# Two cross-attention layers on one core: the scores of a group issued ahead of the maxima in each slot

## The chip, the cores and the metric

The kernel runs on one core of a Trainium2 chip. The metric is the device time of one execution in microseconds. A core has engines that run side by side, each with its own in-order queue: TensorE (PE in the profile, its weight loads PEld), VectorE (DVE), ScalarE (ACT), GpSimd (POOL), and SyncE (SP), which issues most DMAs. They wait for each other by semaphores. Results of TensorE land in PSUM, which the kernel uses as eight banks of 128 partitions by 512 fp32 values, and are read from there by ScalarE or VectorE.

## The reference

Two residual cross-attention layers on the same hidden states, 32 samples of 256 rows by 320 channels, with 77 context rows of 512 channels and 20 heads of 16 channels. In the shapes at hand the layers' object, other and image-prompt parts are cut out of an empty rest of the context, so that what is left of each layer is:

```python
q = heads(x @ wq); k = heads(ctx @ wk); v = heads(ctx @ wv)   # 20 heads of 16
s = einsum('bhqd,bhkd->bhqk', q, k) / sqrt(16)
p = softmax(s, axis=-1)
x = merge(einsum('bhqk,bhkd->bhqd', p, v)) @ wo + bo + x
```

All of it is fp32.

## The kernel before

**Units and groups.** A unit is one layer for one pair of samples: 16 pairs, two layers, 32 units (`units_in_order`). A unit's 20 heads by 2 samples are worked through in five groups of eight (`NG = 5`, g = 0 to 4); the channels stand on the partitions, so a group's scores come out with the 77 keys on the partitions.

**The steps of a unit,** with the names that the profile uses for their tiles:
- `queries` and `outputs_and_queries` (tiles psq, and psy for the output projection of the unit three before), `keys` and `keys_rest` (psk), `vals` (psv): projections. `mask_keys`, `split_keys`, `split_queries` prepare operands on POOL; `spread_keys` and `spread_queries` move them over the partitions by DMA (kS, qs).
- `maxima`: the row maximum for the softmax. TensorE computes scores with the queries on the partitions (psm, line 500; four banks for up to three halves of a group), VectorE reduces each bank (m, line 512). Each unit has ten halves. They are computed some slots ahead of the scores of the same unit, so the maxima of a slot belong to a later unit than its scores.
- `turn`: the ten halves' maxima are split in high and low parts and transposed on VectorE (maxes, mT, lines 532 to 535), then spread by DMA into `max_rows`.
- `scores`: four banks pss. First a matmul that subtracts the maxima (line 550, written "less" below, `pss<-max_rows,less`), then sixteen with the split keys and the queries (line 558), then four exponentials on ScalarE (pT, line 564).
- `values`: `products` multiplies the exponentials of a group with the values (po, line 578, one bank); `divide` transposes po on VectorE (turned, line 590), takes the reciprocal of the sums (inv, line 594) and multiplies on POOL (normal, line 599). `turn_back` transposes the result into oT on VectorE (line 613).
- `add` (line 620) adds bias and residual on VectorE.

**The ring of banks.** All PSUM tiles come from one pool of eight buffers with one tag, in the order of the calls of `bank`. A tile takes the buffer of the tile eight allocations earlier, and its first matmul waits until that one has been read.

**The order.** The order of the instructions is written out by hand. `at(slot, where, step)` notes a step for a slot; at the end the slots are gone through one by one, and in each slot the kinds of step in the order of a tuple; every engine's queue follows this order. Slots 0 to 134 hold the groups: `slot_of(u, g)` gives the slot of a group's scores, its values stand in the slot behind, and its transpose back (g below 4) one later. Four units take 17 slots; units 1, 2 and 3 of each four have their groups 0 and 1 in one slot (a two-score slot), the fourth has one group in its first slot. The maxima are dealt out in order to the slots with a single group: three halves a slot, two in two slots of each 17, none in the two-score slots. Projections of keys and values ("rest" and "full") stand behind the values, one or two in most slots; I call what stands behind po its tail. The paired output and query projection stands at the end of a unit's first slot. Slots below zero are the start-up.

Of the kernel before, what the change touches and what calls it, by code (L numbers as in the profile page):

```python
# [95 lines left out]
def xattn_kernel(ctx: ExitStack, tc: tile.TileContext, xT, cT, cP, weights, outT):  # L96
# [566 lines left out]
    def slot_of(u, g):  # L663
        if u == NU - 2:
            return start(u) + (g + 1) // 2
        if u == NU - 1:
            return start(u - 1) + 3 + g // 2
        return start(u) + (max(0, g - 1) if u % 4 else g)
# [10 lines left out]
    for u, (p, layer) in enumerate(units):  # L679
# [38 lines left out]
        for g in range(NG):  # L718
            slot = slot_of(u, g)
# [65 lines left out]
    for u, slot in ((1, 1), (2, 4)):  # L785
# [7 lines left out]
    at(3, "load", lambda: load_weights(1, "v", "v", nc.sync))  # L793
    at(4, "load", lambda: load_weights(1, "o", "b", nc.sync))

    order = (
        "load", "maxima", "turn back", "scores", "values", "rest", "back", "turn", "split", "full", "last",
    )
    for slot in range(min(s for s, _ in place), max(s for s, _ in place) + 1):
        for where in order:  # L800
            for step in place.get((slot, where), ()):
                step()

# [97 lines left out]
```

## Time and profile before

| | |
|---|---|
| median of 3 runs | 944.42 us (943.32 to 945.34) |
| the profiled execution | 947.08 us |
| its span in the profile | 945.3 us |
| mean granted TensorE clock in it | 0.998 |
| instructions | 48848 |
| matmuls | 21582 |
| VectorE reductions of the maxima, mean | 512, 551 ns |
| ScalarE exponentials, mean | 640, 593 ns |
| VectorE transposes of po, mean | 160, 684 ns |
| VectorE transposes back, mean | 160, 431 ns |

A row of the profile's timeline gives the start and the length in us, the engine, the line, the operation, out<-in, its shape, how many instructions are merged in it, and in brackets the idle time ahead of it with what ended it. A row of the waits gives "engine line waited for: us in total, times, longest". The ends of matmuls are modelled and overlap, so the distance between the starts of successive matmuls says more about TensorE than their lengths; four matmuls on different rows or columns of the array start within 0.02 us and run side by side.

### The profile page before, as it was taken

To read this page: it belongs to the slowest core of one execution; us is meant where nothing else is said; L and a number is where in the kernel's file an instruction comes from. 1 tells how busy PE (TensorE), PEld (TensorE's weight loads), DVE (VectorE), ACT (ScalarE), POOL (GpSimd) and SP (SyncE) were. 2 spreads that over 40 slices of the span, in tenths; PEclk is the share of its full clock that TensorE was granted. 3 is DMA by queue.
4 is the path that set the end of the run, shared out by engine and by line. 5 is a ranking of instruction groups with operands and counts; after the bars stand their busy time and mean duration, and the time that the engine had idled before them with its cause. 6 is when DMAs were issued, how large, how long until landed. Compare 5 with 4: busy or idle time off the path is not lost.

```text
span 945.3 us, 48848 instructions
## 1 busy us (share of the span) xinstructions
PE 926.6 (98%) x21582; PEld 640.8 (68%) x21582; DVE 574.5 (61%) x1330; ACT 432.0 (46%) x975; POOL 406.9 (43%) x608
## 2 busy tenths in 40 slices
PE   8999999999999999999999999999999999999998
PEld 6666667766667666666766677666767666676654
DVE  4475557655577565665656666665566654776575
ACT  2254443644435534355443545335454354444462
POOL 2354445434455434455234454344553335543431
PEclk9999999999999999999999999999999999999999
DMA  6664444253453525536245352355433543353342
GB/s 227 196 217 129 133 147 145 82 172 120 163 153 95 197 76 163 165 104 201 68 145 176 98 201 82 125 175 161 153 96 120 160 155 119 92 162 105 118 136 97
DMA packets 114740, 133.03 MB, mean 141 GB/s; under 512 B 47012, under 2 KB 76004, under 8 KB 114530
## 3 DMA queue, kind: packets, MB, share of 16 engines
q1 hardware_dynamic: 113666, 127.42, 42.8%
q8 instruction: 170, 2.79, 1.3%
q10 hardware_dynamic: 864, 2.49, 0.7%
q14 instruction: 40, 0.33, 0.1%
HBM read 35.39 MB, written 10.49 MB: 49 GB/s over the span
## 4 chain that ended last, share of the span: by engine, by line
PE 88%; DVE 7%; DMA 2%; SPq 1%; issue 1%; POOL 0%; ACT 0%; POOLq 0%
PE psy L203 15%; PE po L578 15%; PE psq L203 14%; PE psm L500 10%; PE psv L203 7%; PE pss L558 7%; PE psk L203 7%; PE psy L237 4%; PE pss L550 4%; PE psq L237 3%; DVE m L512 3%; DVE turned L590 1%; PE psk L344 1%; DVE maxes L533 1%; SPq L316 1%; DMA x<-in_xT_dram 1%
## 5 line engine op out<-in xcount | busy, mean ns | idle before, releaser
L564 ACT ACTIVATE pT<-pss 77x512 f32<-77x512 f32 x640 | 324.4, 593 | 171.7 <-PE pss L558 171.0
L512 DVE TENSOR_REDUCE m<-psm 128x6 f32<-128x462 f32 (+2 forms) x512 | 248.3, 551 | 221.4 <-PE psm L500 220.9
L599 POOL TENSOR_TENSOR normal<-turned,inv 128x256 f32<-128x256 f32 x160 | 99.3, 621 | 484.5 <-DVE inv L594 457.5
L578 PE MATMUL po<-pT,v 77*32 77x256 f32 x2560 | 166.8, 385 | 8.3 <-DVE m L512 5.2
L203 PE MATMUL psy<-oT,w 128*32 128x256 f32 (+1 forms) x3072 | 164.5, 379 | 0.0
L203 PE MATMUL psq<-x,w 128*32 128x256 f32 (+1 forms) x3072 | 153.4, 380 | 0.6 <-DMA w<-in_w_dram 0.6
L203 PEld LDWEIGHTS psy<-oT,w 128*32 128x32 f32 (+1 forms) x3072 | 88.4, 108 | 63.4 <-issue 15.2
L590 DVE STREAM_TRANSPOSE turned<-po 128x512 f32<-128x512 f32 x160 | 109.5, 684 | 24.4 <-PE po L578 24.3
L203 PEld LDWEIGHTS psq<-x,w 128*32 128x32 f32 (+1 forms) x3072 | 86.8, 109 | 54.9 <-issue 2.2
L274 POOL TENSOR_SCALAR kT<-kR,masks 128x154 f32<-128x154 f32 x186 | 113.3, 619 | 19.2 <-ACT kR L333 19.2
L578 PEld LDWEIGHTS po<-pT,v 77*32 77x32 f32 x2560 | 72.4, 109 | 69.6 <-DVE m L512 26.7
L500 PE MATMUL psm<-kT,q 32*128 32x154 f32 x2560 | 116.2, 306 | 2.3 <-POOL kT L274 2.0
L500 PEld LDWEIGHTS psm<-kT,q 32*128 32x128 f32 x2560 | 90.1, 183 | 35.3 <-issue 25.3
L279 POOL TENSOR_TENSOR halves<-q,halves 128x512 fp32r<-128x512 f32 (+1 forms) x93 | 102.1, 1098 | 7.8
L558 PE MATMUL pss<-qs,kS 32*77 32x256 f32 x2560 | 104.6, 276 | 0.0
L620 DVE SCALAR_TENSOR_TENSOR x<-psy,w,x 128x256 f32<-128x256 f32 x160 | 68.3, 476 | 50.6 <-PE psy L203 49.2
L558 PEld LDWEIGHTS pss<-qs,kS 32*77 32x77 f32 x2560 | 89.2, 141 | 11.3
L613 DVE STREAM_TRANSPOSE oT<-normal 128x256 f32<-128x256 f32 x160 | 67.0, 431 | 45.8 <-POOL normal L599 45.8
L203 PE MATMUL psv<-w,cv 128*32 128x160 f32 x2432 | 93.5, 299 | 0.2 <-DVE m L512 0.2
L418 ACT COPY q<-psq 128x256 f32<-128x256 f32 x28 | 10.4, 372 | 161.8 <-PE psq L237 161.8
L203 PEld LDWEIGHTS psv<-w,cv 128*32 128x32 f32 x2432 | 77.8, 110 | 4.4 <-DVE m L512 0.6
L550 PE MATMUL pss<-max_rows,less 32*77 32x512 f32 x640 | 78.7, 468 | 1.4 <-DMA max_rows<-mT 1.4
(48 smaller groups left out, 725.3 us busy)
## 6 DMA issues: line engine op xcount, KB each, us to landing
qs<-halves SPq DMA_DIRECT2D x256, 128.0 KB
kS<-k_halves SPq DMA_DIRECT2D x128, 192.5 KB
c<-in_cP_dram SPq DMA_DIRECT2D x32, 308.0 KB
cv<-in_cT_dram SPq DMA_DIRECT2D x38, 256.0 KB
out_dram<-x SPq DMA_DIRECT2D x15, 640.0 KB
x<-in_xT_dram SPq DMA_DIRECT2D x14, 640.0 KB
qs<-halves SPq DMA_DIRECT2D x128, 64.0 KB
v<-stage SPq DMA_DIRECT2D x26, 192.5 KB
```

The costliest lines, as they stand in the source:

```text
L203: nc.tensor.matmul(out[m : m + 32], lhsT[:, m : m + 32], rhs, **flags)
L274: engine.tensor_scalar_mul(kT[:, e], kR[:, groups], masks[:, e : e + 1])
L279: engine.tensor_tensor(low, x, high.bitcast(F32), ALU.subtract)
L500: nc.tensor.matmul(ps[j][:, i * 2 * L : (i + 1) * 2 * L], q[r, c * P : (c + 1) * P], kT[r, :, g % 2, :], start=True, stop=True,)
L512: nc.vector.tensor_reduce(st[u]["m"].rearrange("p e h j -> p h e j")[:, first : first + n, :, j], ps[j][:, at * 2 * L : (at + n) * 2 * L]. ...
L550: nc.tensor.matmul(ps[j][:L], less[r, g % 4, :], max_rows[u % 2][r, g // 4], start=True, stop=False)
L558: nc.tensor.matmul(ps[j][:L, e * S : (e + 1) * S], st[u]["ks"][r, e, g, half, :], q[r, :], start=False, stop=(half == 1 and e == 1),)
L564: nc.scalar.activation(st[u]["p", g][j][:L], ps[j][:L], AF.Exp, scale=SCALE)
L578: nc.tensor.matmul(po[o : o + 32, e * S : (e + 1) * S], vpad[:L, b, pair, e].rearrange("p a d -> p (a d)"), pT[j][:L, e * S : (e + 1) * S] ...
L590: nc.vector.transpose(turned[:, 0 : 2 * S], po)
L599: nc.gpsimd.tensor_tensor(normal.rearrange("p q e d -> p e q d"), outs, inv.unsqueeze(3).broadcast_to([P, 2, S // 32, HD]), ALU.mult,)
L620: nc.vector.scalar_tensor_tensor(x, ps[:, 0:S], w_sb[layer]["b"][:, 0, t : t + 1], x, ALU.add, ALU.add)
```

## The change

In every slot above 0 the kind "scores" is taken ahead of "maxima" and "turn back"; it stood behind both. Slots up to 0 keep the old order. No instruction is added or removed.

```diff
-    order = (
+    first_order = (
         "load", "maxima", "turn back", "scores", "values", "rest", "back", "turn", "split", "full", "last",
     )
+    order = (
+        "load", "scores", "maxima", "turn back", "values", "rest", "back", "turn", "split", "full", "last",
+    )
     for slot in range(min(s for s, _ in place), max(s for s, _ in place) + 1):
-        for where in order:
+        for where in order if slot > 0 else first_order:
             for step in place.get((slot, where), ()):
                 step()
```

On TensorE a slot was maxima, scores, values, tail; it is scores, maxima, values, tail. The allocations of banks go 4 (pss), 4 (psm), 1 (po) in place of 4 (psm), 4 (pss), 1 (po). On VectorE the order within a slot stays reductions, transposes back, transpose of po and reciprocal. On ScalarE, POOL and SP nothing changes place.

## The prediction

> **What bounds the kernel now.** I read the page first, its busy shares and the chain that ended last:
>
> ```profile
> PE 926.6 (98%) x21582; PEld 640.8 (68%) x21582; DVE 574.5 (61%) x1330; ACT 432.0 (46%) x975; POOL 406.9 (43%) x608
> PE 88%; DVE 7%; DMA 2%; SPq 1%; issue 1%; POOL 0%; ACT 0%; POOLq 0%
> ```
>
> TensorE is both the busy engine and the chain; whatever delays its in-order queue is paid in full. But 98% is the union of overlapping matmuls and hides gaps between *starts*, so I read next who the weight loads (PEld) wait for:
>
> ```profile
> PEld po L578 <- DVE m L512: 26.7, 89, 1.1
> PEld po L578 <- ACT pT L564: 7.1, 26, 0.3
> PEld po L578 <- PE pss L558: 4.7, 14, 0.3
> ```
>
> The repeated stop is ahead of the values (po): 89 times behind a reduction of the maxima, 26 times behind an exponential. Last, the timeline of one three-half slot with a short tail, and the two-score slot behind it (start, length):
>
> ```profile
> 208.53 1.07 PE L500 MATMUL psm<-kT,q 32*128 32x154 f32 x24
> 209.32 0.51 PE L550 MATMUL pss<-max_rows,less 32*77 32x512 f32 x4
> 209.62 0.64 DVE L512 TENSOR_REDUCE m<-psm 128x6 f32<-128x462 f32 x1 [1.08 <-PE psm L500]
> 209.62 2.28 DVE L512 TENSOR_REDUCE m<-psm 128x6 f32<-128x462 f32 x4 [1.08 <-PE psm L500]
> 209.66 0.65 PE L558 MATMUL pss<-qs,kS 32*77 32x256 f32 x16
> 210.32 1.07 PE L578 MATMUL po<-pT,v 77*32 77x256 f32 x16
> 211.21 1.24 PE L203 MATMUL psk<-c,w 128*32 128x154 f32 x32
> 211.82 0.43 DVE L613 STREAM_TRANSPOSE oT<-normal 128x256 f32<-128x256 f32 x1
> 212.18 0.67 DVE L590 STREAM_TRANSPOSE turned<-po 128x512 f32<-128x512 f32 x1
> 212.37 0.46 PE L550 MATMUL pss<-max_rows,less 32*77 32x512 f32 x4
> 213.14 0.40 PE L550 MATMUL pss<-max_rows,less 32*77 32x512 f32 x4
> 213.37 0.64 PE L558 MATMUL pss<-qs,kS 32*77 32x256 f32 x16
> 213.40 0.59 ACT L564 ACTIVATE pT<-pss 77x512 f32<-77x512 f32 x1 [0.60 <-PE pss L558]
> 214.04 1.07 PE L578 MATMUL po<-pT,v 77*32 77x256 f32 x16
> ```
>
> What it shows is the ring of eight PSUM banks: each tile waits until the tile eight allocations earlier has been read out. Maxima take 4 banks, scores 4, po 1. In the first slot po stands eight behind the first maxima bank: that reduction ends at 210.26, po starts 0.05 us later. In the second slot (two sets of scores, no maxima) po stands eight behind the first score bank: its exponential ends at 213.99, po starts 0.05 us later. So the 0.05 us is the hand-over, and the second slot is a measured picture of what every slot becomes when scores go first.
>
> **What moves on TensorE.** L is the first matmul of the scores. From the two-score slot, L to last score matmul is 213.03 − 212.37 = 0.66; then 0.37 until the exponential starts, 0.59 for it, 0.05: po at L + 1.67, at the earliest, whatever the maxima take. On TensorE the maxima now fill this time: a start after the scores of 0.105 (row: second less after scores; no row shows scores then maxima, the nearest are 0.08, less to maxima at start-up, and 0.31, queries to maxima), a stream of 0.68 (six groups 0.13 apart; today 0.785, its first group filling an empty array), and 0.22 to po (row: maxima to psv at start-up 0.22; scores to po without a wait 0.20): 0.66 + 0.105 + 0.68 + 0.22 = 1.66. Hidden, just, by the 1.67. Today's length from first maxima matmul to po, slot by slot, is set against 1.67:
> - three halves, ordinary: 208.53 to 210.32, 1.79; gain 0.12
> - three halves of two units (eight shorter reductions): 226.14 to 228.03, 1.90; gain 0.23
> - the slot behind a turn of the maxima, where VectorE comes 0.5 late to the reductions: 231.52 to 233.74, 2.22; gain 0.55
> - two halves: 291.33 to 292.77, 1.44; loss 0.23, for the exponential's path is the longer one now
> - two sets of scores, no maxima: nothing.
>
> The step into the slot (0.22 to 0.31 by what went before) is the same with maxima or scores first: the double slots pay 0.222 behind psk as the others do. No DMA is moved, and neither SP's, POOL's nor ScalarE's order changes; scores need max_rows and qs some slots after their DMAs, and starting 0.8 earlier leaves these covered.
>
> **What moves on VectorE.** Its order stays (reductions, transposes back, transpose of po, reciprocal), but it cannot begin before the maxima, which now end 0.22 before po instead of 1.0. First reduction: 0.30 after the last maxima matmul, so po + 0.09, today po − 0.70: all behind it is 0.79 later against po. The transpose of po ended at 212.85, po + 2.53; it will end at po + 3.32, and with two transposes back (205.40 to 208.25 today, 2.86) at po + 3.65. Queued behind the reductions are the transposes back and po's own; who waits for these is the ring and the output projection:
>
> Slot with psk alone behind po, next a two-score slot: the third bank of its second scores is po's. It is wanted at po + 2.83 (213.15 − 210.32), free at 3.32 + 0.05. Today there are 0.24 us to spare, then 0.54 are missing. Restart from there: 0.29 to the first score matmul, 0.36, 0.20, po at 4.22 against 3.72. Loss 0.48 (two such slots in 17).
>
> Same slot, next one with three halves: its third maxima bank is po's, wanted at 2.05 + 0.66 + 0.105 = 2.82, free at 3.37; then 0.785 + 0.22, po at 4.37 against 3.72. Loss 0.65.
>
> Behind a turn: the chain of copies for the maxima (1.71 us) ends 0.85 after the next po, that slot's reductions start there, its po is transposed 3.51 later, and the bank (the slot has psk and psv behind po) is wanted 0.44 earlier. Its own restart costs 0.53 (twice).
>
> One unit in four starts in a slot with maxima, and the output projection follows po directly:
>
> ```profile
> 270.84 1.07 PE L578 MATMUL po<-pT,v 77*32 77x256 f32 x16
> 271.73 1.70 PE L203 MATMUL psy<-oT,w 128*32 128x256 f32 x28
> 272.34 0.43 DVE L613 STREAM_TRANSPOSE oT<-normal 128x256 f32<-128x256 f32 x1
> ```
>
> The fourth group's oT is wanted after three steps of 0.43, po + 0.89 + 1.30 = 2.19; it is there at po + 1.93 today, 2.77 after: loss 0.58. Two-half slots: where the slot before has three halves and psv alone, po's bank delays the maxima to a further loss of 0.33; their own reductions are short (1.64), and cause none.
>
> **The sum** over the 17 slots of four units (first at 198.3 to 312.1), in order: +0.12, +0.12, +0.12, −0.48, +0.23, +0.55, 0.12 − 0.53, −0.48, +0.23, +0.55, 0.12 − 0.53, 0.12 − 0.65 − 0.58, +0.12, +0.12, −0.23 − 0.33, −0.23, 0 = −1.5 us: gains 2.5, costs 4.0. Seven such stretches: −10.8. Two have a second psv that hides the 0.33: +0.7. Start-up (−0.5), one slot behind a turn without psv (−0.6) and the end (−0.2), by the same rules: −1.3. In all 11.4 us longer: span 945.3 to 956.7, that execution (947.08, 1.8 outside the span) to 958.5. The median before, 944.42, lies 0.3% below its profiled run; I add to the median: 955.8.
>
> A rule is weighed here. The row first: four reductions take 2.28 us of what TensorE makes in 0.79. The Trainium skill, "TensorEngine Tiling (Array Packing)", section "PSUM Bottleneck", says that tiling speeds TensorE but not the emptying of PSUM, which may then become the limit. Before, the trace hardly bears it out: only one 0.05 us hand-over behind a transpose of po, at 60.14 in the start-up, reaches TensorE. By the rule the costs above stand (+11 us); by the quiet rows of before alone they don't (−14 us).
>
> **The rivals.** (1) Slower by less than its gains, that is *faster*: one mechanism, po's bank comes free in time. It decides where VectorE's chain behind the reductions ends 0.5 us earlier against po than worked out (or TensorE's tail is as much longer). Then of 4.0 only the two-half slots' 0.46 is left: 2.5 − 0.46 = 2.0 in 17 slots, 14 us, 930. For it: before, VectorE is 61% busy and no such wait shows. Against: the 0.79 shift follows from the order itself, and the spare time today is 0.24. If half of the cost comes, the result is no change. (2) Scores to maxima costs 0.31, as queries to maxima, not 0.105: 0.2 more in some nine slots of 17 and as much on the stalls they feed, 9 to 13 us on top, 965 to 969. Against: less behind scores, the same 32-row shape, costs 0.105. A gain on that term buys nothing, since the exponential's 1.67 stands. (3) The change does nothing: the wait before po passes from reduction to exponential with the same length and stalls eat the 0.12s: 944. It would need both at once.
>
> **How the numbers follow.** A measurement of this kernel tells about 0.2% (1.9 us) from no change. Forecast, stalls as worked out within a third: 0.74, 948 to 962. (2): 0.12. (3) or half the stalls: 0.05. (1): 0.09. All of the first two are slower: 0.86. The range takes the forecast's and the lower part of (2): 947 to 965, leaving out (1), (3) and the top of (2).
>
> **What would show it.** Right: po waits for ACT pT about 130 times instead of 26, and for DVE m hardly; L to po is 1.67 in two- and three-half slots alike; waits of pss and psm for "turned" appear, some 0.5 us each, and one of psy for oT seven times; reductions start about 0.1 after po. Wrong: po waiting longer than 1.67 behind L (the exponential is late), no wait for turned (rival 1), or scores to maxima well above 0.1 (rival 2).

## The result and the profile after

The changed kernel takes 955.2 us, median of 4 runs (954.41 to 956.82), against 943.87 us of the kernel before in the same comparison (943.26 to 945.34, 4 runs): 1.012 times as long, 95% interval 1.0101 to 1.0138. Its profiled execution took 955.1 us. The two spans, 953.3 and 945.3, differ by 8.0 and not by 11.3, since the profiled execution of before lost 3.6 us in the start-up, on the same instructions; from slot 1 on the changed kernel is 11.6 us longer.

I count slots modulo 17 below: slot 0 holds the first group of the fourth unit, slots 5, 9 and 13 are the two-score slots, slots 3 and 4 have two halves of maxima, slots 11 and 15 stand behind a turn, and slots 10 and 14 hold a turn and the maxima of two units (slots 0 and 4 hold the other two turns). The page's busy shares and its chain that ended last:

```profile
PE 936.6 (98%) x21582; PEld 641.8 (67%) x21582; DVE 573.5 (60%) x1330; ACT 435.7 (46%) x975; POOL 407.2 (43%) x608
PE 87%; DVE 9%; DMA 1%; ACT 1%; SPq 1%; POOL 0%; issue 0%; POOLq 0%; ACTq 0%
```

TensorE is as "busy" as before, for its stalls hide in the union of overlapping matmuls; the chain tells more: VectorE's share has gone from 7% to 9%. The view of waits (engine, line, waited for: us in total, times, longest):

```profile
PEld po L578 <- ACT pT L564: 22.7, 109, 0.5
PEld psm L500 <- DVE turned L590: 6.0, 18, 1.0
PEld pss L550 <- DVE turned L590: 5.9, 15, 0.5
PEld psy L203 <- DVE oT L613: 4.6, 7, 0.7
PEld psm L500 <- ACT stage L442: 2.5, 2, 1.5
```

The row "po <- DVE m", 89 times in the kernel before, has gone: po waits for an exponential instead. In its place stand the waits for "turned", the transpose of po, and for oT. The weight loads' idle time contains an ordinary step of 0.2 to 0.25, so it is the count that matters here, not the total. Rows of the timeline of the two slots that the prediction showed (start, length, engine, line, operation, how many; in brackets the idle time and what ended it):

```profile
206.65 0.46 PE L550 MATMUL pss<-max_rows,less 32*77 32x512 f32 x4
207.41 0.96 PE L500 MATMUL psm<-kT,q 32*128 32x154 f32 x24
208.33 1.07 PE L578 MATMUL po<-pT,v 77*32 77x256 f32 x16
208.41 2.28 DVE L512 TENSOR_REDUCE m<-psm 128x6 f32<-128x462 f32 x4 [0.97 <-PE psm L500]
210.96 0.67 DVE L590 STREAM_TRANSPOSE turned<-po 128x512 f32<-128x512 f32 x1
211.15 0.99 PE L550 MATMUL pss<-max_rows,less 32*77 32x512 f32 x4
211.69 0.14 PEld L550 LDWEIGHTS pss<-max_rows,less 32*77 32x77 f32 x1 [0.51 <-DVE turned L590]
```

In the three-half slot po starts 1.68 behind the first score matmul (206.65 to 208.33), and the reductions 0.08 behind po, where they stood 0.70 ahead of it. In the two-score slot the four matmuls of "less" no longer start together: the bank of the last is po's of the slot before, its transpose ends at 211.63, and its weights go at 211.69, 0.54 behind the first. Both are the numbers of the prediction, which had the third bank in the place of the fourth.

### The profile page after: what moved, and what is told of

It is laid out like the page before. It is cut to its first block, busy times and chain, and to the rows that moved or that the text cites. A ratio compares the mean times of both kernels' runs of the same rounds, so it can differ in the third digit from the quotient of the medians.

```text
span 953.3 us, 48845 instructions
## 1 busy us (share of the span) xinstructions
PE 936.6 (98%) x21582; PEld 641.8 (67%) x21582; DVE 573.5 (60%) x1330; ACT 435.7 (46%) x975; POOL 407.2 (43%) x608
## 4 chain that ended last, share of the span: by engine, by line
PE 87%; DVE 9%; DMA 1%; ACT 1%; SPq 1%; POOL 0%; issue 0%; POOLq 0%; ACTq 0%
PE psy L203 14%; PE psq L203 14%; PE po L578 14%; PE psm L500 9%; PE pss L558 7%; PE psv L203 7%; DVE m L512 7%; PE psk L203 6%; PE pss L550 6%; PE psy L237 4%; PE psq L237 4%; PE psk L344 2%; DVE turned L590 1%; DVE oT L613 1%; ACT pT L564 1%; DMA v<-stage 1%
## 5 line engine op out<-in xcount | busy, mean ns | idle before, releaser
L500 PE MATMUL psm<-kT,q 32*128 32x154 f32 x2560 | 118.9, 294 | 5.9 <-POOL kT L274 2.1
L578 PEld LDWEIGHTS po<-pT,v 77*32 77x32 f32 x2560 | 69.5, 109 | 58.9 <-ACT pT L564 22.7
L500 PEld LDWEIGHTS psm<-kT,q 32*128 32x128 f32 x2560 | 99.3, 183 | 13.2 <-DVE turned L590 6.0
L558 PE MATMUL pss<-qs,kS 32*77 32x256 f32 x2560 | 107.3, 277 | 0.0
L203 PE MATMUL psk<-c,w 128*32 128x154 f32 x2048 | 79.8, 297 | 0.5 <-DVE m L512 0.5
```

What stands on the lines that cost most here:

```text
L203: nc.tensor.matmul(out[m : m + 32], lhsT[:, m : m + 32], rhs, **flags)
L500: nc.tensor.matmul(ps[j][:, i * 2 * L : (i + 1) * 2 * L], q[r, c * P : (c + 1) * P], kT[r, :, g % 2, :], start=True, stop=True,)
L558: nc.tensor.matmul(ps[j][:L, e * S : (e + 1) * S], st[u]["ks"][r, e, g, half, :], q[r, :], start=False, stop=(half == 1 and e == 1),)
L578: nc.tensor.matmul(po[o : o + 32, e * S : (e + 1) * S], vpad[:L, b, pair, e].rearrange("p a d -> p (a d)"), pT[j][:L, e * S : (e + 1) * S] ...
```

## The experiments

Each kernel is the changed one with its loop line altered. In all but two of them (named below) only some slots, modulo 17, have the scores ahead, and the rest, with all slots up to 4, keep the old order. The line that replaces this one is shown, with what else is changed:

```diff
-        for where in order if slot > 0 else first_order:
```

Ratios are against the kernel before on the same chip (median 944.68 us for the first eight, 944.33 for the last two).

**The gain alone, behind a turn.**

```diff
+        for where in order if slot > 4 and slot % 17 in (11, 15) else first_order:
```

> Scores ahead of the maxima only in slots 11 and 15 of each 17 (those behind a turn of the maxima), the old order elsewhere. Theory (ring of banks): here the values no longer wait for a reduction that VectorE begins 0.5 us late, and VectorE's later chain meets a long tail (psk and psv), so nothing is lost behind them. Ten such slots gain 0.55 us each, the ones with two psv 0.12, and slot 113, which gains 1.0, gives it back at its short tail: some 5.9 us faster, 938 against 943.9, ratio 0.994. In the profile the 0.72 gaps ahead of po shrink to 0.22. Rival (the cost of scores first is spread evenly over all slots, some 0.1 us in each of the 110 with maxima, from array refills and later reductions): 14 slots, 1.4 us slower, ratio 1.0015.

Measured: 938.37 us (937.53 to 940.89), ratio 0.9935 [0.9917, 0.9952]. L to po is 1.66 to 1.68 in all these slots but one (2.03 in slot 83, counted from the start, where the maxima's own matmuls stop, as they do in the kernel before). The gain is real and of the predicted size; what the whole change loses is lost in other slots.

**The slots without a stall behind them.**

```diff
+        for where in order if slot > 4 and slot % 17 in (1, 6, 7, 11, 15) else first_order:
```

> Scores first only in slots 1, 6, 7, 11 and 15 of each 17: all whose tail is long enough for VectorE's later chain and which start no output projection. Theory: the 5.9 us of slots 11 and 15, and 0.12 in each of 21 more slots, 2.5: 935.5, ratio 0.991. No wait for a transpose of po behind these slots. Rival (cost spread evenly): 35 slots by 0.1, 3.5 us slower, ratio 1.004.

Measured: 936.63 us (934.51 to 936.78), ratio 0.9904 [0.9885, 0.9923]: faster than both kernels. Its view of waits:

```profile
PEld po L578 <- ACT pT L564: 13.7, 63, 0.3
PEld po L578 <- DVE m L512: 12.9, 52, 1.2
```

Po waits for the exponential in some of the slots and for the reductions in the rest; no row of psm waiting for "turned" appears. In the slots with the new order L to po is 1.66 to 1.68 but for slot 66 (2.34), where a score bank waits for ScalarE's reading of psv. The expectation of no wait for a transpose of po fails once: behind slot 113, whose tail has no psv, the scores of slot 114 wait 0.90 for "turned" and lose 0.89, as the expectation of the first experiment said.

**The cost ahead of a two-score slot.** Slot 8 alone, a three-half slot with a short tail:

```diff
+        for where in order if slot > 4 and slot % 17 == 8 else first_order:
```

> Scores first only in slot 8 of each 17 (psk alone behind po, then a slot with two sets of scores). Theory: slot 8 gains 0.11, and the slot behind loses 0.50 because the third bank of its second scores is that of po, which VectorE transposes 0.79 us later against po: 0.39 by seven, and 0.2 at the end, 2.9 us slower, 946.8, ratio 1.003. In the profile the second scores of slot 9 stop for 0.54 us, 0.05 behind the end of a transpose of po. Rival (cost spread evenly): 8 slots by 0.1, 0.8 us slower, ratio 1.001, no such stop.

Measured: 947.3 us (946.16 to 949.66), ratio 1.003 [1.0019, 1.0041]. Its timeline at the two-score slot:

```profile
210.65 0.67 DVE L590 STREAM_TRANSPOSE turned<-po 128x512 f32<-128x512 f32 x1
210.83 0.99 PE L550 MATMUL pss<-max_rows,less 32*77 32x512 f32 x4
```

The second scores of that slot start at 210.83, but the last of their four "less" (merged into a row of 0.99) comes behind the transpose, whose end is at 211.32. L to po of the two-score slot is 2.16 to 2.17 for 1.67. One slot in 17, with a gain of its own of 0.12, makes the kernel slower.

**The same slot with VectorE's chain shortened.** That "turned" is the cause could still be a coincidence of times. Slot 8 again, with the transposes back ahead of the reductions, so that the transpose of po ends 0.3 earlier:

```diff
-        "load", "scores", "maxima", "turn back", "values", "rest", "back", "turn", "split", "full", "last",
+        "load", "scores", "turn back", "maxima", "values", "rest", "back", "turn", "split", "full", "last",
...
+        for where in order if slot > 4 and slot % 17 == 8 else first_order:
```

> As the kernel with scores first only in slot 8 of each 17, but in that slot the transpose back stands ahead of the reductions on VectorE, which idles there. Theory: po's transpose comes 0.35 us earlier, so the stop of the next slot's second scores falls from 0.54 to 0.19 us, and its loss from 0.50 to 0.15; with the 0.11 gained in slot 8, 0.04 by seven: no change, ratio 1.000 to 1.001 (1.003 without it). Rival (the stop has another cause, the reductions' own banks or ScalarE): the stop stays at 0.54 and the ratio at 1.003.

Measured: 944.28 us (942.85 to 946.77), ratio 0.9998 [0.9986, 1.001]. Its timeline at the two-score slot:

```profile
209.48 0.71 DVE L590 STREAM_TRANSPOSE turned<-po 128x512 f32<-128x512 f32 x1
210.03 0.67 PE L550 MATMUL pss<-max_rows,less 32*77 32x512 f32 x4
211.10 1.07 PE L578 MATMUL po<-pT,v 77*32 77x256 f32 x16
```

The transpose ends at 210.19, and the second "less" start within 0.22 and not 0.54. L to po of the two-score slot is 1.84 to 1.85. The slots and the matmuls with their order are the same, only VectorE's order is another (po's bank goes to the third score tile here, to the fourth there, but both wait for the same transpose), and the loss follows it: the wait for "turned" is the cost.

**The cost in the output projection.** Slot 0 alone:

```diff
+        for where in order if slot > 4 and slot % 17 == 0 else first_order:
```

> Scores first only in slot 0 of each 17, the slot with one group and the paired output and query projection behind its values. Theory: the slot gains 0.12, but the transpose back of the fourth group stands behind the reductions and comes 0.58 us too late for the projection's fourth step, and the additions come later by as much behind the turn (0.17 more): 0.63 by seven, 4.4 us slower, ratio 1.0047. In the profile psy stops once in each of the seven, 0.05 behind the end of a transpose back. Rival (cost spread evenly, 0.1 a slot): 0.7 us slower, ratio 1.001.

Measured: 949.04 us (947.44 to 951.6), ratio 1.0048 [1.003, 1.0066]. Timeline and wait:

```profile
271.92 0.43 DVE L613 STREAM_TRANSPOSE oT<-normal 128x256 f32<-128x256 f32 x1
272.40 0.85 PE L203 MATMUL psy<-oT,w 128*32 128x256 f32 x12 [0.40 <-DVE oT L613]
```

```profile
PEld psy L203 <- DVE oT L613: 6.1, 7, 0.9
```

The fourth group's matmuls start when their oT ends. In all seven projections 5.07 for 4.47 pass from the first matmul of psy to the first of the queries behind it, 0.60 longer (predicted: 0.58).

**The two-half slots.**

```diff
+        for where in order if slot > 4 and slot % 17 in (3, 4) else first_order:
```

> Scores first only in slots 3 and 4 of each 17, which have two halves of maxima. Theory: po then waits for the first exponential, 1.67 us from the first score matmul where two halves of maxima and the scores took 1.44 in the old order: 0.23 by 14, 3.2 us slower, ratio 1.0034; no wait for a transpose of po, since two halves are reduced 0.6 us sooner. Rival (cost spread evenly): 1.4 us slower, ratio 1.0015, and the distance from scores to po follows the number of maxima (1.40).

Measured: 947.36 us (945.98 to 950.47), ratio 1.0031 [1.0018, 1.0043]. L to po is 1.66 to 1.68 in all 14 slots, where maxima to po took 1.44.

**What the 1.67 consists of.** Two kernels add to the last one, for the groups 3 and 4 of each fourth unit. One does the fourth exponential once more, ahead of the four (it computes the same):

```diff
-        for j in range(4):
+        for j in (3, 0, 1, 2, 3) if u % 4 == 0 and u > 0 and g > 2 else range(4):
```

> As the kernel with scores first only in slots 3 and 4 of each 17, but in these slots the fourth exponential is done once more ahead of the four. Theory, mended after the reversed order (the values take the bank that is read first, and wait for that reading): the first bank to come free is again the first score bank, now read 0.48 us later, so po stands 2.15 us behind the first score matmul instead of 1.67: 0.48 by 14, 6.7 us on top of the 2.9, ratio 1.010. Rival (po waits for the scores' matmuls or TensorE's refill, the exponential is hidden): ratio 1.003, po at 1.67.

Measured: 954.97 us (952.75 to 957.38), ratio 1.0112 [1.0094, 1.0129]. Its timeline:

```profile
290.69 0.64 PE L578 MATMUL po<-pT,v 77*32 77x256 f32 x8 [0.77 <-ACT pT L564]
```

Po waits longer, for ScalarE, and L to po is 2.16 or 2.17 in slot 4 and 2.22 or 2.23 in slot 3 (2.50 in one of the seven). An exponential in the row takes ScalarE 0.48, from start to start, and in slot 4 all of it, 0.50, passes to po; the 0.07 more in slot 3 were not followed up. The exponential's chain, not the matmuls, sets L to po. The median is 7.6 us above the two-half kernel's, 0.54 for each of the 14 slots. The other kernel does the four in reverse order:

```diff
-        for j in range(4):
+        for j in (3, 2, 1, 0) if u % 4 == 0 and u > 0 and g > 2 else range(4):
```

> As the kernel with scores first only in slots 3 and 4 of each 17, but in these slots the four exponentials are done in the reverse order, so that the first score bank is read last. Theory: po waits for the bank eight allocations earlier, the first score bank, whose exponential now ends three times 0.477 us later: from first score matmul to po 3.10 us instead of 1.67, 1.43 by 14, 20 us on top of the 3.2: 968 against 944.5, ratio 1.025. Rival (po waits for the scores' matmuls, the maxima or TensorE's own refill, and the exponential only happens to end there): no more than the 3.2, ratio 1.0034.

Measured: 948.85 us (948.15 to 950.3), ratio 1.0048 [1.0031, 1.0066]: a miss. L to po is 1.69 to 1.71 in 13 of the 14 slots (1.97 in slot 122), not three exponentials longer. Po still waits for an exponential, but for the one that is done first:

```profile
291.06 0.64 PE L578 MATMUL po<-pT,v 77*32 77x256 f32 x8 [0.23 <-ACT pT L564]
```

The banks written in that program say why: po has the bank of the *fourth* score tile there, allocated five before and read first. So "the tile eight allocations earlier", said ahead of the prediction and in it, is no rule. The banks fit a pool that hands out the one that is released first in the planned order. In the kernel before, where readings follow allocations, this is as good as a ring: 1704 of 1739 allocations stand eight behind the last one of their bank; in the changed one it is 1452, with 149 at seven, 101 at nine and 22 at eleven. The corrected theory is that po waits for the score bank read *first*, whichever it is. By it the reversed order leaves L to po as in the two-half kernel; it was 0.03 longer there, and the intervals of the two ratios overlap.

**An unpredicted wait behind two turns.** In slots 50 and 63 of the changed kernel (counted from 0 as in the code; the expectations below call them 49 and 62) the maxima take 2.16 and 2.63 from first to last matmul, not 0.68. Rows of the timeline of the changed kernel in slots 49 and 50 (SPq is SyncE's issuing of DMAs):

```profile
375.39 3.51 SPq L537 DMA_DIRECT2D max_rows<-mT  x4
379.00 2.53 SPq L485 DMA_DIRECT2D v<-stage  x3
381.43 0.49 ACT L442 COPY stage<-psv 128x160 f32<-128x160 f32 x2 [3.31 <-DMA v<-stage]
381.78 1.25 PE L500 MATMUL psm<-kT,q 32*128 32x154 f32 x20 [0.78 <-ACT stage L442]
```

The chain runs from the bottom up: the maxima wait for ScalarE to read the bank of psv; ScalarE waits for a stage buffer, which the DMAs of v have not yet read; these wait on SyncE's queue behind the DMAs of the turn of slot 48, and the turn ends later since VectorE does. Counted from the start of slot 49, the DMAs of the turn begin at 1.48 (0.59 in the kernel before), take 3.51 to issue (2.70), and v's begin at 5.09 (3.39). So about half of the 1.7 by which v's DMAs are late is VectorE's later end, and most of the rest is the slower issue behind it. Two edits test the chain; these are the two kernels that keep the new order elsewhere. The first takes the turn behind the projections of kind "full" in slots 10 and 14, and all else as in the changed kernel:

```diff
+    turn_last = (
+        "load", "scores", "maxima", "turn back", "values", "rest", "back", "split", "full", "turn", "last",
+    )
...
+        for where in first_order if slot <= 0 else turn_last if slot % 17 in (10, 14) else order:
```

> The changed kernel, with the turn of the maxima behind the steps of kind full in slots 10 and 14 of each 17, so that SP issues the copies of the values (v from stage) ahead of the spreading of the maxima. Theory: in the changed kernel the maxima of slots 49 and 62 stop for 1.3 to 1.5 us because ScalarE's copy of psv waits for v-from-stage copies that stand on SP's queue behind the four DMAs of a turn that VectorE now ends later; with this order both stops go, 2.8 us of the 11.3 lost: 952.4, ratio 1.009 against the kernel before. Rival (the stop comes from the ring alone, ScalarE's copy being needed earlier because scores take less time than maxima did): no change against the changed kernel, 955.2, ratio 1.012.

Measured: 957.03 us (953.96 to 958.17), ratio 1.0118 [1.0097, 1.014]: no gain over the changed kernel, the rival's number and a miss of the theory's. The stop of the maxima was taken away as meant (0.68 and 0.67 in slots 50 and 63), which the rival did not allow, but the max_rows, now later on the queue, came too late for the scores of slot 64:

```profile
474.06 0.46 PE L550 MATMUL pss<-max_rows,less 32*77 32x512 f32 x4 [2.85 <-DMA max_rows<-mT]
```

The cause was there, and its time went to the next wait: slot 63 is 0.97 longer than in the changed kernel, though its maxima take 1.96 less. The second edit leaves SyncE's order alone and gives only slots 48 and 61, whose turns are meant, the old order, so that VectorE comes earlier to them:

```diff
+        for where in order if slot > 0 and slot not in (48, 61) else first_order:
```

> The changed kernel with the old order in slots 48 and 61 alone, the two slots with a turn of the maxima whose following slot has two psv. Theory: there the turn ends 0.9 us sooner, SP issues its four DMAs and the copies of the values behind them sooner, ScalarE's copy of psv is free in time, and the stops of the maxima in slots 49 and 62 (2.16 and 2.63 us from first to last maxima matmul instead of 0.68) go: 3.4 us less, 0.4 of gains lost, so 3.0 less than the changed kernel: 952.2, ratio 1.0088. Rival (the stops come from the scores being issued earlier in slots 49 and 62 themselves): the stops stay, ratio 1.012.

Measured: 952.19 us (950.89 to 952.84), ratio 1.0074 [1.006, 1.0087]. The DMAs of the turn and of v are issued earlier:

```profile
374.94 2.70 SPq L537 DMA_DIRECT2D max_rows<-mT  x4
377.74 2.82 SPq L485 DMA_DIRECT2D v<-stage  x3
```

Counted from the start of slot 49 again, the turn's begin at 0.58 and v's at 3.38, as in the kernel before, and the maxima of slots 50 and 63 take 0.74 and 0.92. The ratio's interval lies below the changed kernel's: 1.4 and 1.7 us of its loss are this chain.

## Why the prediction was right, and where its steps were off

The forecast, the sign and the mechanism hold: the time lies 0.6 us below the 955.8 (the change is 11.3 us, 11.4 were forecast), VectorE's chain behind the reductions is what comes too late, and the gain and the three costs, each taken alone, have the sizes that were worked out. The other terms of the table, the restarts of slots 12 and 16 and po's late bank in slot 3 among them, were not tried alone; they are read from the trace. Slot by slot, the stretch of slots 23 to 39 (the lengths in the kernel before less those in the changed one; + is a gain):

| slots | kind | predicted | measured |
|---|---|---|---|
| 6, 7, 8, 1, 2 | three halves, ordinary | +0.12 each | +0.11 to +0.13 |
| 10, 14 | of two units | +0.23 | +0.23, +0.22 |
| 11, 15 | behind a turn | +0.55 | +0.56, +0.55 |
| 9 | two scores, behind a short tail | −0.48 | −0.50 |
| 12, 16 | restart behind a turn | −0.41 | −0.42, −0.39 |
| 4 | two halves | −0.23 | −0.23 |
| 3 | two halves, po's bank late | −0.56 | −0.55 |
| 13 | two scores, behind stalled maxima | −0.48 | −0.29 |
| 0 | three halves, behind a short tail | −0.53 | −0.29 |
| 0 | oT for the output projection | −0.58 | −0.38 |
| 0 | queries behind it | 0 | −0.17 |
| sum | | −1.5 | −1.07 |

**Two slips in the sum.** Po at 4.22 against 3.72 is a loss of 0.50, not 0.48; 0.50 was measured. And −1.5 by seven is −10.5 to −10.6 from the printed terms, not −10.8.

**L to po, 1.67.** Right in every slot that isn't stalled (1.66 to 1.68), in two- and three-half slots alike. Po waits for the exponential 109 times, where about 130 were named (the view's 11 at the matmuls are the same waits again).

**Scores to maxima, 0.105.** The rows of before had no such step. It is 0.105 in the median of 106 places of the changed kernel (0.083 to 0.161): the nearest row by shape was the right one, and rival 2 with its 0.31 falls. Maxima to po is 0.222, as taken.

**VectorE's shift, 0.79, and what waits for it.** Right where a slot's maxima run unstalled: reductions 0.08 behind po, the wait for po's bank 0.54, oT at +0.60 when slot 0 is changed alone. Rival 1, po's bank free in time, falls: 33 waits for "turned" at psm and pss, where the kernel before has only seven at pss, of an ordinary step's length, and the slot-8 kernel is slower. With a change clear of noise rival 3 falls too.

**The chained stalls: over-sized.** In slots 13 and 0 I added the full shift again behind a slot that is itself stalled. The timeline of the changed kernel in the stalled slot 12:

```profile
235.35 1.51 PE L500 MATMUL psm<-kT,q 32*128 32x154 f32 x24
236.67 2.28 DVE L512 TENSOR_REDUCE m<-psm 128x6 f32<-128x462 f32 x4 [0.63 <-PE psm L500]
236.79 1.07 PE L578 MATMUL po<-pT,v 77*32 77x256 f32 x16
```

The reductions start 0.12 *ahead* of po here, not 0.09 behind. TensorE stops at the third bank, from 235.49 to 235.81, when the first half is done in two banks. These two stay a step ahead: their last matmuls start at 236.33, those of the other two at 236.58, and VectorE starts on the first bank while TensorE still makes the last. A stall thus gives VectorE back 0.2 of its delay. In slot 0 this shows as 0.29 and 0.38 in place of 0.53 and 0.58; changed alone, behind a slot without a stall, it cost the full 0.60. The terms add up to 0.63 per stretch too much (0.19 + 0.24 + 0.20), less the 0.17 of the queries: about 3.2 us over seven stretches. The 0.17 is a step with no cost in my sum. In the changed kernel's view of waits the queries wait for an addition seven times, and in the view of before never:

```profile
PEld psq L203 <- DVE x L620: 1.1, 7, 0.2
```

The additions stand behind the turn on VectorE. The expectation for slot 0 alone named this cost, and its slots lose 0.66 or 0.67 each (0.60 + 0.17 − 0.12 is 0.65); in slot 102 of the changed kernel, where the additions come 0.43 sooner, it is gone. No run moves the additions alone.

**"No DMA is moved, and neither SP's, POOL's nor ScalarE's order changes."** The order stands, its times don't. The step left out that the turn's own DMAs wait for VectorE, and that v's DMAs are queued behind them on SyncE: 3.1 us in slots 50 and 63 that no step of mine had. This miss and the over-sized chained stalls are of one size and opposite sign, so that the sum is closer than its terms is luck. Seven stretches are 10.5 us longer (predicted 10.7: 10.8 less the 0.7 of the second psv, and the 0.6 behind slot 113, which lies in the last stretch and measured 1.05). Slots 1 to 5 lost 1.1 (predicted 0.5; not followed up) and the end nothing (predicted 0.2). All behind the start of slot 1 is 11.6 us longer (predicted 11.4).

**The rule on PSUM.** The prediction says that the trace of before hardly bears the rule out. That is a misreading: its own row of 89 waits of po for a reduction of the maxima is TensorE waiting until PSUM is emptied. The Trainium skill, "TensorEngine Tiling (Array Packing)", section "PSUM Bottleneck", bears on both kernels. What the runs add is that here the place of the reader in VectorE's order decides, and not how busy VectorE is (574.5 us before, 573.5 after): with the same eight banks the two-score slot loses 0.54 or 0.22 between its "less" matmuls as the transposes back stand behind or ahead of the reductions. "Perfetto Trace Analysis", section "Identifying Performance Opportunities", says that the same gap repeated for a stretch of the kernel on the engine that should be full can mean too few buffers in PSUM; the runs here show repeated gaps that an order of the readers, at the same number of buffers, made or made shorter.

## What to carry to other kernels

When work on a full engine is reordered to fill a wait, cost every slot with the consumer's clock too: here 0.12 to 0.55 us per slot were won on TensorE, and VectorE, 60% busy on average, was made 0.79 later against po and took back more wherever the next slot was short. Such a change need not be taken whole: with the spare time between a bank's release and its next use known for each kind of slot, the new order in the slots that have enough of it brought 0.96% where the new order everywhere cost 1.2%. And a step whose place in a DMA queue is unchanged can still hold up what stands behind it, if the engine that feeds it became later.

## What was not expected of the hardware

SyncE's issuing is not even. The four DMAs of max_rows took 2.70 us to issue behind the turns of slots 48 and 61 in the kernel before and in the one with the old order in these slots; in the changed kernel, where they begin 0.9 later, they took 3.51 and 3.41. The three DMAs of v behind them took 2.45 to 2.82. With some 0.7 to 0.9 us each, a queue of seven is 5.5 to 6 us long, enough to make a delay of a microsecond on VectorE a wait of TensorE two slots on. Why the same issues differ by up to 0.2 us each stays open.
